# Attention's last units in an attention and feed-forward kernel: the division by the maxima in three steps, and the last norms' shift as a step of its own

## The chip, the cores and the metric

The kernel runs on one core of a Trainium2 chip. The metric is the device time of one launch in microseconds (us). The core has five engines that work side by side, each through its own instructions in order: TensorE (PE, matmuls), VectorE (DVE), ScalarE (ACT), GpSimd (POOL) and SyncE (SP), of which the last issues most of the transfers.

## The reference

Four sequences of 1024 tokens with 256 features go through attention with 16 heads of 16 features, and then through a gated feed-forward block of width 1024. Each half is normalised before and after, and added to its input.

```python
x = x + _layernorm(_L0_attn_ref(_layernorm(x, axis=-1), L0_attn_Wqkv, L0_attn_Wout), axis=-1)
x = x + _layernorm(_L0_ffn_ref(_layernorm(x, axis=-1), ...), axis=-1)

# attention's softmax
x_max = jax.lax.stop_gradient(jnp.max(x, axis=-1, keepdims=True))
exp_x = jnp.exp(jnp.clip(x - x_max, -50.0, 50.0))
return exp_x / (jnp.sum(exp_x, axis=-1, keepdims=True) + EPS)

# feed-forward
h = jax.nn.silu(_tlin(x, w1_w, w1_s)) * _tlin(x, w2_w, w2_s)
h = jax.nn.gelu(_tlin(h, h1_w, h1_s), approximate=False)
h = jax.nn.gelu(_tlin(h, h2_w, h2_s), approximate=False)
return _tlin(h, w3_w, w3_s)
```

The kernel takes the exponential of the scores without subtracting the maximum. The maximum enters only through the small EPS (1e-6) of the denominator, which must then be scaled by the largest exponential of a row: den = EPS * (largest exponential) + (sum of exponentials).

## The kernel before, in words

**Attention's units.** The work of attention is cut into 4 sequences x 4 groups of 4 heads x 2 halves of 512 queries: 32 units. A unit has 16 tiles: 8 blocks c of 128 keys, with two tiles u of two heads each. For a tile, two matmuls make the scores in a PSUM buffer `s` (L536; there are three such buffers, and the feed-forward's `pg` and `ph` use the same three), and ACT takes the exponential into a ring of SBUF buffers `e` (L537). The ring holds 8 tiles, that is 4 blocks c. `weigh` (L544) multiplies the exponentials by the values into one PSUM buffer `acc`, four matmuls for a block; a block may be cut into two halves of 256 queries. `rise` (L556) keeps the running maximum of the exponentials of a unit in `top` on VectorE, for 128 of the 512 queries: the first of a unit reads blocks 0 and 1, each later one a further block, seven in all. A part of the ring is written again only when both `weigh` and `rise` have read it.

**The end of a unit.** `unit_end` (L795) transposes `acc` into `o` (L798) and hands the division to a list of work on the side. `divide` sends the maxima through DRAM to turn them. The two units of the last sequence's last group take `divide_last` (L599) instead, which turns and folds the maxima on VectorE alone, in one step: a transpose (`turned`, L605), a reduction (L606), four small copies (L609), a reduction (L611), four small copies (`em`, L615), and the four instructions of `quotients` (L563 to L567), which end in the normalised heads `on`.

**The ending of half a sequence.** `ending` (L620) is what follows the last group of a half: two transposes to `oT` (L629), two products with the output weights, `py` (L321), each copied to `y`, then the norm of y (statistics, and `root` with POOL's power), its application and the residual's addition. In the last sequence the application is ACT's, which needs `nb`, the shift, made by VectorE in `shift` (L117) at the head of the first `apply`. All `py` use one PSUM buffer, `misc`. Behind the projections of half 1 stands `open_ffn`, which opens the feed-forward's memory.

**The list on the side.** There is no scheduler behind this: the order of every engine's instructions is the order in which the Python code emits them. The main loop emits scores, exponentials, maxima and weighings by the turn (three tiles at a time), and after each turn calls `take`, which walks through chains of steps. A `Step(run, gap, tensor, heavy, work)` may run when `gap` turns have passed since the last step of its chain; one with `work` also needs that much room on VectorE left in this turn; only one step with matmuls runs in a turn.

```python
while (step := self.due(chain, self.slot, free)) and (step.tensor or not step.work or self.room > spare):
```

**The first part of the feed-forward.** After the last unit, `gated` (L954) emits 16 groups, 8 for each half of the first sequence: eight `pg` matmuls (L966), ACT's `sg` (L968) and VectorE's `g` (L969), which frees the PSUM buffer. For the first sequence `take` is called after each group, so that attention's last steps are emitted between the groups; after the eighth everything that `open_ffn` waits for is emitted at once:

```python
steps[7].append(lambda: until(lambda: "fb" in ffn))
```

From there on, steps of the feed-forward split `g` into two parts for the next layer, `hi` on ACT (L936) and `lo` on VectorE (L940), and the `ph` matmuls (L1045) follow after group 16.

Of the kernel before, what the change touches and what calls it, by code (L numbers as in the profile page):

```python
# [19 lines left out]
P = 128  # L20
HEADS = 16
DH = 16
SLOT = 32
HPG = P // SLOT
# [15 lines left out]
TPQ = NQ // P  # L40
# [41 lines left out]
class Norms:  # L82
# [30 lines left out]
    def shift(self, stats, n=TPQ):  # L113

        mv, rstd = stats
        nb = self.small.tile([P, TPQ], F32, tag="nb", name="nb", bufs=self.bufs)
        self.nc.vector.scalar_tensor_tensor(nb[:, :n], mv[:, :n, 0], -1.0, rstd[:, :n], ALU.mult, ALU.mult)  # L117
        return rstd, nb
# [11 lines left out]
def tile_fast(ctx: ExitStack, tc: tile.TileContext, x, wqk, wv, wo, w1, w1s, w2, w2s, h1, h1s, h2, h2s, w3, w3s, out, bad):  # L130
    nc = tc.nc
    B, S, D = x.shape
# [4 lines left out]
    NH = S // NQ  # L137
# [34 lines left out]
    norms = Norms(nc, const, small)  # L172
# [23 lines left out]
    with ExitStack() as actx, ExitStack() as rctx:  # L196
# [59 lines left out]
        work = actx.enter_context(tc.tile_pool(name="work", bufs=2, side="right"))  # L256

        def misc(name):
            return ps_misc.tile([P, NQ], F32, tag="misc", name=name)
# [58 lines left out]
        def by_slots(o, w, i, **flags):  # L318

            for j in range(0, P, SLOT):  # L320
                nc.tensor.matmul(o[j : j + SLOT, :], w[:, j : j + SLOT], i, **flags)  # L321
# [236 lines left out]
        def quotients(g, h, em, o):  # L558

            o = o.rearrange("p (j s) -> p j s", s=SLOT)  # L560
            den = small.tile([P, NQ // SLOT], F32, tag="den", name="den")
            n = P // SLOT
            nc.vector.scalar_tensor_tensor(den[:, 0:n], em, SM_EPS, o[:, 0:n, DH], ALU.mult, ALU.add)  # L563
            nc.vector.tensor_copy(den[:, n:], o[:, n:, DH])
            nc.vector.reciprocal(den, den)
            e = DH * (g % GPT)
            nc.vector.tensor_mul(on[h][:, g // GPT, :, e : e + DH], o[:, :, 0:DH], den.unsqueeze(2).to_broadcast([P, NQ // SLOT, DH]))  # L567
# [31 lines left out]
        def divide_last(g, h, o, top):  # L599


            def run():
                turned = work.tile([P, P // SLOT, P], F32, tag="folded", name="turned", bufs=1)
                flat, n = top.rearrange("p u n q -> p (u n q)"), HPG * P // SLOT
                nc.vector.transpose(turned.rearrange("p s q -> p (s q)"), flat)  # L605
                nc.vector.tensor_reduce(flat[:, 0:n], turned.rearrange("p s (j k) -> p (s j) k", k=SLOT), AX.X, ALU.max)  # L606
                parts = flat[0:SLOT, n : n + n * P // SLOT].rearrange("p (k n) -> p k n", n=n)
                for k in range(P // SLOT):
                    nc.vector.tensor_copy(parts[:, k], flat[SLOT * k : SLOT * (k + 1), 0:n])  # L609
                most = flat[0:SLOT, P : P + n]  # L610
                nc.vector.tensor_reduce(most, parts.rearrange("p k n -> p n k"), AX.X, ALU.max)  # L611
                most = most.rearrange("p (i j) -> p i j", i=HPG)
                em = small.tile([P, P // SLOT], F32, tag="em", name="em")
                for i in range(HPG):
                    nc.vector.tensor_copy(em[SLOT * i : SLOT * (i + 1), :], most[:, i])  # L615
                quotients(g, h, em, o)

            return [Step(run, 1, False)]

        def ending(b, h, copy):  # L620

            st = {}

            def transposes(c):
                def run():
                    if c == 0:
                        st["oT"] = work.tile([P, DC, NQ], F32, tag="oT", name=f"oT_{b}_{h}", bufs=1)
                        st["y"] = (both if h else work).tile([P, TPQ, D], F32, tag="y", name=f"y_{b}_{h}", bufs=1)
                    nc.vector.transpose(st["oT"][:, c, :], on[h][:, c].rearrange("p j s -> p (j s)"))  # L629

                return run

            def project(t0):
                def run(*parts):
                    if 0 in parts:
                        st["py"] = misc(f"py_{b}_{h}_{t0}").rearrange("p (t d) -> p t d", d=D)
                    py = st["py"]
                    for i in parts:
                        for c in range(DC):
                            by_slots(py[:, i, :], st["oT"][:, c, (t0 + i) * P : (t0 + i + 1) * P], wo_sb[:, c, :], start=c == 0, stop=c == DC - 1)  # L640
                    if 1 not in parts:
                        return
                    (copy if b == B - 1 else to_scalar)(st["y"][:, t0 : t0 + 2, :], py)

                return run

            def gather(i):
                def run():
                    st["mv"] = norms.gather([st["y"][:, j, :] for j in range(i, i + 2)], i, st.get("mv"))

                return run

            def root():
                st["ln"] = norms.root(st["mv"])

            def apply(i0):
                def run():
                    if b == B - 1 and i0 == 0:
                        st["to"] = norms.shift(st["ln"])
                    for i in range(i0, i0 + 2):  # L660
                        if b == B - 1:
                            norms.scale(st["y"][:, i, :], st["y"][:, i, :], st["to"], i)
                        else:
                            norms.apply(st["y"][:, i, :], st["y"][:, i, :], st["ln"], i)

                return run

            def residual(i):
                def run():
                    xr = xs[b][:, h * TPQ + i : h * TPQ + i + 2, :]  # L670
                    nc.vector.tensor_add(xr, xr, st["y"][:, i : i + 2, :])

                return run

            steps = [Step(transposes(c), 1, False, work=0.7) for c in range(DC)] + [Step(lambda run=project(t): run(0, 1), 2, heavy=True) for t in range(0, TPQ, 2)]
            before = (b, h - 1) if h else (b - 1, NH - 1)
            steps[0].ready = lambda: before not in ends or not any(step.tensor for step in ends[before][0])
            tail = (
                [Step(gather(i), 1, False, work=1.6) for i in range(0, TPQ, 2)] + [Step(root, 0, False, work=0.3)]
                + [Step(apply(i), 2 if b == B - 1 and not i else 1, False, work=1.2) for i in range(0, TPQ, 2)] + [Step(residual(i), 1, False, work=1) for i in range(0, TPQ, 2)]  # L680
            )
            if b < B - 1:

                return steps + [Step(lambda: side.add(tail), 0, False)]
            opened = Step(open_ffn, 0, False)
            opened.ready = lambda: not ends[b, 0][0]
            return steps + ([opened] if h == NH - 1 else []) + tail
# [107 lines left out]
        def unit_end(b, g, h):  # L795
# [7 lines left out]
            if g == NG - 1:  # L803
                last = ending(b, h, to_scalar if (b, h) == (B - 1, NH - 1) else to_vector)
                unit[0].extend(last)
                ends[b, h] = unit
# [429 lines left out]
        def feed_forward():  # L1236
# [27 lines left out]
            for b in range(B):  # L1264
# [25 lines left out]
                until(lambda: made_factors[0] == len(corners) and "fb" in ffn)  # L1290
                q = 2 * 7 * b
                ops, extra, early = ending(one, False)
                if b == 0:
                    for g in range(3, 12):
# [8 lines left out]
                until(lambda: not chain[0])  # L1303
                two = Layer(y, ops[0, 0], ops[1, 0])
                ops, extra, early = ending(two, True)
                if b:
                    checked(extra, (3, 4), (5, 6))
# [79 lines left out]
        while weighed < len(tiles):  # L1387
            n = end = made
# [3 lines left out]
            if made == len(tiles):  # L1392
                n = made
# [8 lines left out]
            while halves and weighed + 2 <= n:  # L1402
                b, g, h, c, _ = tiles[weighed]
# [264 lines left out]
```

## Time and profile before

| | |
|---|---|
| three runs, us | 1205.09, 1205.70, 1208.14 (median 1205.7) |
| the profiled execution, us | 1206.14, of which the span from first to last instruction is 1204.4 |
| busy share of the span | TensorE 96%, ACT 74%, VectorE 70%, POOL 25% |
| granted TensorE clock, mean | 0.994 |
| last exponentials of attention | end at 576.7 us |
| first pg matmul | 577.7 us |
| first ph matmul | 617.8 us |

The profile is one execution. A line such as L556 names the kernel's line whose instruction it is. In the groups, `out<-in` are the program's names of the tiles. Idle time of an engine is put down to the instruction that ended it. The matmuls are pipelined, so their single durations overlap.

### The profile page before, as it was taken

How to read it: one execution, taken by the hardware profiler on the slowest of the kernel's cores; microseconds unless marked ns; L12 is line 12 of the kernel's file. 1: busy time of each engine (PE TensorE's matmuls, PEld its weight loads, DVE VectorE, ACT ScalarE, POOL GpSimd, SP SyncE). 2: the span in 40 equal slices, each digit the busy share in tenths (PEclk: the TensorE clock that was granted, in tenths of full speed). 3: DMA queues.
4: the chain of work that ended last, by engine and by line, in shares of the span. 5: the costliest groups of instructions: out<-in, count | busy, mean ns of one | idle time of the engine just before them, and what ended most of it. 6: DMA issues, size and time to landing. Idle time of an engine off the chain costs nothing.

```text
span 1204.4 us, 21320 instructions
## 1 busy us (share of the span) xinstructions
PE 1160.6 (96%) x7994; PEld 709.1 (59%) x7994; DVE 845.9 (70%) x1501; ACT 886.2 (74%) x1050; POOL 298.7 (25%) x458
## 2 busy tenths in 40 slices
PE   8999999999999999998999999999999999999994
PEld 3333333333333333332678889888898888988884
DVE  4577777785878867767585756867678676785765
ACT  4999888988999989998466575576756767567660
POOL 6454256565566643220000000000000000000000
PEclk9999999999999999999999999999999999999997
DMA  5877655676666664472314441354522545225401
GB/s 144 214 185 185 150 134 157 163 178 163 155 175 164 167 166 105 106 176 88 105 36 140 134 147 57 101 175 153 179 74 85 177 154 176 74 84 187 157 24 38
DMA packets 78672, 163.66 MB, mean 136 GB/s; under 512 B 14688, under 2 KB 40928, under 8 KB 78560
## 3 DMA queue, kind: packets, MB, share of 16 engines
q1 hardware_dynamic: 62832, 120.18, 34.9%
q0 software_dynamic: 15200, 41.50, 12.6%
q8 instruction: 65, 1.06, 0.4%
q10 hardware_dynamic: 528, 0.52, 0.1%
q14 instruction: 47, 0.39, 0.1%
HBM read 98.71 MB, written 29.88 MB: 107 GB/s over the span
## 4 chain that ended last, share of the span: by engine, by line
PE 71%; DVE 10%; ACT 9%; issue 4%; DMA 3%; SPq 2%; POOL 1%; ACTq 0%; POOLq 0%; DVEq 0%
PE ph L1045 35%; PE acc L544 10%; PE pg L966 9%; ACT e L537 8%; PE s L536 7%; PE pz L1153 4%; PE p L321 2%; DVE top L556 2%; PE py L321 2%; SPq L482 1%; PE pv L321 1%; DVE st L97 1%; DMA x<-in_x_dram 1%; DMA sq<-cq0hi 1%; PE fpt L909 1%
## 5 line engine op out<-in xcount | busy, mean ns | idle before, releaser
L537 ACT ACTIVATE e<-s 128x1024 f32<-128x1024 f32 x512 | 483.0, 1046 | 43.8 <-PE s L536 34.1
L544 PE MATMUL acc<-e,vaug 128*32 128x512 f32 (+1 forms) x2424 | 256.6, 535 | 1.4 <-DVE o L798 1.4
L107 POOL TENSOR_TENSOR rstd<-ve,minus_half 128x4 f32<-128x4 f32 (+1 forms) x34 | 38.3, 1126 | 700.6 <-DVE ve L105 596.2
L536 PE MATMUL s<-sq,sk 64*128 64x512 f32 x1024 | 188.9, 445 | 20.7 <-ACT e L537 19.5
L536 PEld LDWEIGHTS s<-sq,sk 64*128 64x128 f32 x1024 | 87.3, 184 | 167.9 <-ACT e L537 147.4
L1045 PE MATMUL ph<-hi,sq 128*128 128x512 f32 x448 | 177.8, 397 | 0.0
L1045 PE MATMUL ph<-lo,sq 128*128 128x512 f32 x448 | 176.7, 394 | 0.0
L1045 PE MATMUL ph<-hi,sk 128*128 128x512 f32 x448 | 176.6, 394 | 0.0
L1045 PE MATMUL ph<-lo,sk 128*128 128x512 f32 x448 | 176.5, 394 | 0.0
L556 DVE TENSOR_TENSOR top<-top,e 128x512 f32<-128x512 f32 x192 | 140.1, 730 | 21.1 <-ACT e L537 15.4
L544 PEld LDWEIGHTS acc<-e,vaug 128*32 128x32 f32 x2424 | 61.9, 109 | 117.4 <-issue 107.4
L940 DVE TENSOR_TENSOR lo<-g,hi 128x1024 fp32r<-128x1024 f32 x48 | 58.8, 1224 | 57.8 <-ACT hi L936 57.8
L1045 PEld LDWEIGHTS ph<-lo,sk 128*128 128x128 f32 x448 | 84.1, 188 | 20.0
L1045 PEld LDWEIGHTS ph<-hi,sk 128*128 128x128 f32 x448 | 84.1, 188 | 20.0
L1045 PEld LDWEIGHTS ph<-hi,sq 128*128 128x128 f32 x448 | 84.1, 188 | 19.5
L1045 PEld LDWEIGHTS ph<-lo,sq 128*128 128x128 f32 x448 | 84.2, 188 | 19.2
L1033 ACT ACTIVATE c<-ph,h_scale 128x512 f32<-128x512 f32 x64 | 40.5, 684 | 55.8 <-PE ph L1045 55.8
L940 DVE TENSOR_TENSOR lo<-c,hi 128x1024 fp32r<-128x1024 f32 x48 | 58.2, 1219 | 25.8 <-ACT hi L936 25.8
L968 ACT ACTIVATE sg<-pg,w_scale 128x512 f32<-128x512 f32 x64 | 43.9, 687 | 41.6 <-PE pg L966 38.2
L321 PE MATMUL p<-xT,wqk_sb 128*32 128x512 f32 x512 | 65.7, 593 | 0.5 <-ACT xT L324 0.5
L969 DVE SCALAR_TENSOR_TENSOR g<-pg,w_scale,sg 128x512 f32<-128x512 f32 x64 | 47.7, 747 | 22.1 <-ACT sg L968 22.1
L1153 PE MATMUL pz<-w_sb,hi 128*128 128x256 f32 x256 | 60.1, 279 | 0.0
(189 smaller groups left out, 1830.0 us busy)
## 6 DMA issues: line engine op xcount, KB each, us to landing
sq<-h_f SPq DMA_DIRECT2D x56, 512.0 KB, 3.9
sk<-h_f SPq DMA_DIRECT2D x56, 512.0 KB, 4.7
w<-in_h_dram POOLq DMA_DIRECT2D x32, 256.0 KB, 4.9
h_f<-wr POOLq DMA_DIRECT2D x16, 512.0 KB, 3.7
x<-in_h_dram SPq DMA_DIRECT2D x16, 512.0 KB, 3.6
top_d<-top SPq DMA_DIRECT2D x30, 256.0 KB, 2.5
folded<-top_d SPq DMA_DIRECT2D x30, 256.0 KB, 3.6
h_f<-wr POOLq DMA_DIRECT2D x16, 384.0 KB, 3.8
```

What stands on the lines that cost most here:

```text
L321: nc.tensor.matmul(o[j : j + SLOT, :], w[:, j : j + SLOT], i, **flags)
L536: nc.tensor.matmul(s[:, a, :], stacks[1, g % 2, u][r, c * P : (c + 1) * P], stacks[0, g % 2, u][r, h * NQ : (h + 1) * NQ], start=True, sto ...
L537: nc.scalar.activation(pair(k)[:, u], s, AF.Exp)
L544: nc.tensor.matmul(acc[SLOT * i : SLOT * (i + 1), q0:q1], vaug[g % 2][:, c, i, :], pair(k)[:, i // 2, i % 2, q0:q1], start=c == 0 and q0 = ...
L556: nc.vector.tensor_max(top, top if c > 1 else pair(k - 2)[:, :, :, 0:P], pair(k)[:, :, :, 0:P])
L940: nc.vector.tensor_sub(self.lo[i].t, self.raw[i].t, self.hi[i].t.bitcast(F32))
L966: nc.tensor.matmul(p[:, k, :], homes[n][d][:, m * P : (m + 1) * P], half[:, d, :], start=d == j == 0, stop=d == DC - 1 and j == 1)
L968: nc.scalar.activation(sg, p[:, 0, :], AF.Silu, scale=scales["w1"][:, m : m + 1])
L969: nc.vector.scalar_tensor_tensor(x[i, h][c // 2].t[:, c % 2, :], p[:, 1, :], scales["w2"][:, m : m + 1], sg, ALU.mult, ALU.mult)
L1033: nc.scalar.activation(o.t[:, j, :], (o.t if src is None else src)[:, j, :], AF.Gelu, scale=scale[:, m : m + 1])
L1045: nc.tensor.matmul(p[:, j, :], w, half, start=start and c == n == 0, stop=c == HC // 2 - 1 and n == 1, skip_group_check=True,)
L1153: nc.tensor.matmul(p[:, j, :D], half[:, (t0 + j) * P : (t0 + j + 1) * P], homes["w3"][c], start=c == order[0] and n == 0, stop=c == order[ ...
```

## The change

Two things are changed. First, `divide_last` returns three steps in place of one: `turn` (transpose and first reduction), `fold` (four copies and second reduction) and `run` (the copies to `em` and the quotients). For half 1 the second and third follow at once; for half 0 each has a gap of one turn and a weight in work. Second, in the last sequence `norms.shift` is a step of its own, `shift`, with a gap of 1 + h turns, and the first `apply` has a gap of 1 in place of 2.

```diff
         def divide_last(g, h, o, top):
-            def run():
+            flat, n = top.rearrange("p u n q -> p (u n q)"), HPG * P // SLOT
+            most = flat[0:SLOT, P : P + n]
+
+            def turn():
                 turned = work.tile([P, P // SLOT, P], F32, tag="folded", name="turned", bufs=1)
-                flat, n = top.rearrange("p u n q -> p (u n q)"), HPG * P // SLOT
                 nc.vector.transpose(turned.rearrange("p s q -> p (s q)"), flat)
                 nc.vector.tensor_reduce(flat[:, 0:n], turned.rearrange("p s (j k) -> p (s j) k", k=SLOT), AX.X, ALU.max)
+
+            def fold():
                 parts = flat[0:SLOT, n : n + n * P // SLOT].rearrange("p (k n) -> p k n", n=n)
                 for k in range(P // SLOT):
                     nc.vector.tensor_copy(parts[:, k], flat[SLOT * k : SLOT * (k + 1), 0:n])
-                most = flat[0:SLOT, P : P + n]
                 nc.vector.tensor_reduce(most, parts.rearrange("p k n -> p n k"), AX.X, ALU.max)
-                most = most.rearrange("p (i j) -> p i j", i=HPG)
+
+            def run():
                 em = small.tile([P, P // SLOT], F32, tag="em", name="em")
                 for i in range(HPG):
-                    nc.vector.tensor_copy(em[SLOT * i : SLOT * (i + 1), :], most[:, i])
+                    nc.vector.tensor_copy(em[SLOT * i : SLOT * (i + 1), :], most.rearrange("p (i j) -> p i j", i=HPG)[:, i])
                 quotients(g, h, em, o)
-            return [Step(run, 1, False)]
+            if h == NH - 1:
+                return [Step(turn, 1, False), Step(fold, 0, False), Step(run, 0, False)]
+            return [Step(turn, 1, False, work=1.4), Step(fold, 1, False, work=1.0), Step(run, 1, False, work=1.7)]
...
+            def shift():
+                st["to"] = norms.shift(st["ln"])
+
             def apply(i0):
                 def run():
-                    if b == B - 1 and i0 == 0:
-                        st["to"] = norms.shift(st["ln"])
                     for i in range(i0, i0 + 2):
...
-                + [Step(apply(i), 2 if b == B - 1 and not i else 1, False, work=1.2) for i in range(0, TPQ, 2)] + [Step(residual(i), 1, False, work=1) for i in range(0, TPQ, 2)]
+                + ([Step(shift, 1 + h, False)] if b == B - 1 else []) + [Step(apply(i), 1, False, work=1.2) for i in range(0, TPQ, 2)] + [Step(residual(i), 1, False, work=1) for i in range(0, TPQ, 2)]
```

In the order of instructions, only the stretch between the last unit's first maximum and the end of the pg groups differs. On VectorE the first maximum of the last unit follows L606, the second and third follow L611, the fourth follows L567; the second `oT` transpose of half 0 follows the first `g`. On TensorE the four `py` products follow pg groups 3, 5, 8 and 8, where they followed groups 1, 3, 6 and 8. On ACT the fourth `hi` (after group 12) stands ahead of half 1's shifts instead of behind them.

## The prediction

> **What bounds the kernel now.** I read the page's busy slices first, then the chain of work that ended last around the place that the change touches, then the timelines of ACT and TensorE there.
>
> ```profile
> PE   8999999999999999998999999999999999999994
> ACT  4999888988999989998466575576756767567660
> ```
>
> TensorE is at nine tenths nearly everywhere, so an edit can gain only where TensorE waits. The one 8 behind the start is the slice from 542 to 572 us, the end of attention; ACT falls from 8 to 4 behind it. There the chain reads (start, us, what):
>
> ```profile
> 563.06 0.63 DVE turned L605
> 563.72 0.70 DVE top L606
> ...
> 565.17 0.26 DVE top L611
> ...
> 567.08 0.69 DVE top L556
> ...
> 568.77 0.72 ACT e L537
> ```
>
> The path to the end runs through the whole of one division (L605 to L567), then through one running maximum (L556), then to ACT's exponentials. The waits of 556 to 612 us name it (us in total, times, longest), and the timelines of ACT and TensorE show both ends (in brackets the idle time before an instruction, and who ended it):
>
> ```profile
> ACT e L537 <- DVE top L556: 3.9, 1, 3.9
> ```
>
> ```profile
> 567.85 5.61 ACT L537 ACTIVATE e<-s 128x1024 f32<-128x1024 f32 x6 [3.92 <-DVE top L556]
> 574.73 1.94 ACT L537 ACTIVATE e<-s 128x1024 f32<-128x1024 f32 x2 [1.27 <-PE s L536]
> ...
> 568.93 0.50 PE L536 MATMUL s<-sq,sk 64*128 64x512 f32 x2 [2.85 <-ACT e L537]
> ```
>
> ACT has filled the ring of eight tiles of e by 563.94. The ninth tile overwrites the first, which the first maximum of the last unit reads; that maximum stands on VectorE behind the 15 instructions of the other half's division. So ACT is idle for 3.92 us, then TensorE, starved of s buffers, for 2.85. Stretches of 1 us (length, then busy us of TensorE, its weight loads, VectorE, ACT and POOL, then the granted clock) show a second price:
>
> ```profile
> 570.00:571.00 1.00, 0.59 (x4) 0.23 (x4) 0.94 (x2) 1.00 (x2) 0.00 (x0) 0.94 0.00 0
> 571.00:572.00 1.00, 1.00 (x10) 0.37 (x12) 0.34 (x1) 1.00 (x2) 0.00 (x0) 0.50 0.06 16
> ...
> 574.00:575.00 1.00, 1.00 (x12) 0.52 (x12) 0.18 (x1) 0.27 (x1) 0.00 (x0) 0.85 0.00 0
> ```
>
> The clock is at half speed from about 570.9 to 574.3. Sixteen weighing matmuls (L544) take 2.79 us there and 1.50 at 564.58, and ACT waits another 1.27 us for s. The last weighing ends and the first pg matmul of the feed-forward starts at 577.77. From there to the first ph matmul at 617.95 is 40.18 us, with TensorE idle in two places:
>
> ```profile
> 611.11 0.51 PE L966 MATMUL pg<-ck1hi,ck0hi 128*128 128x512 f32 x1 [0.96 <-DVE g L969]
> 615.82 0.50 PE L966 MATMUL pg<-ck1hi,ck0hi 128*128 128x512 f32 x1 [0.75 <-DVE g L969]
> ...
> 611.82 1.09 ACT L122 ACTIVATE y<-y,nb,rstd 128x256 f32<-128x256 f32 x2 [2.99 <-DVE nb L117]
> ```
>
> After 617.95 the chain is TensorE alone up to the last few us, so whatever is won or lost before it shifts the end by as much.
>
> **The change part by part.** No instruction is added or removed on any engine, and no DMA is issued by the moved steps; the instruction orders of SP and POOL are as before. Up to the reduction at 563.72 (L606) all engines have the same order, so 0 there. Two stretches differ.
>
> *Part 1, the division of half 0 in three steps.* On VectorE the first maximum of the last unit now follows L606 directly; the next two follow L611; the fourth follows the division. L606 ends at 563.72 + 0.69 = 564.41, so the maximum ends at 564.44 + 0.69 = 565.1 instead of 567.8. Its inputs are there (exponentials done at 563.94), and the other reader of the ring's first pair, the weighing of c = 0, ran at 561.8 to 562.8. ACT restarted 0.09 us after the maximum, so now at 565.2: 2.65 us earlier. The second maximum ends at 565.1 + 0.7 (L609) + 0.3 (L611) + 0.7 = 566.8, the third at 567.5; they free the tiles that ACT wants at 568.9 and 570.7, so neither holds it.
>
> Then eight exponentials. Six took 5.61, that is 0.915 a step, so eight take 7.44 and end at 572.65 if s keeps up. TensorE's order is unchanged: three s tiles, each behind an exponential, the last ending at 568.6; 1.5 us of weighing at full clock to 570.1; the s of the last two tiles by 570.4 and 570.8, against ACT's wish at 570.7 and 571.6. No gap. Before, the last exponential ended at 574.73 + 1.94 = 576.67, so ACT ends 4.0 us earlier. The last weighing follows 1.1 us behind, as before: first pg at 573.7 instead of 577.8. Of the 4.0, 2.65 is the wait and 1.35 is what the half clock cost.
>
> That second term rests on the clock staying up. In the trace the half clock begins 4.8 us after TensorE's pause began, behind a 3.4 us stretch (567.5 to 570.9) in which it was busy for about 1.3 us, 37%. The Trainium skill ("TensorE: Matmul & The Clock Gate", "What's actually happening" and "HAM oscillation — how this bites in real kernels") says that the clock drops to half after at least one idle window of about 3.4 us, and comes back after one busy window. Read strictly, a pause of 2.85 us is too short, the half clock has another cause and stays: then part 1 is worth 2.65. The row speaks for the pause: it dropped in the window that held it, and for 3.4 us. In the new order TensorE is busy about 2.5 of the 3.4 us from 566.1 (1.5 for three s tiles, 0.95 of weighing), 74%, and an earlier row had less without a drop:
>
> ```profile
> 22.00:26.00 4.00, 2.29 (x26) 1.18 (x18) 0.29 (x1) 1.96 (x3) 3.99 (x9) 1.00 0.56 125
> ```
>
> 57% at clock 1.00. I take 4.0 and keep 2.65 as the other end.
>
> *Part 2, the order inside the pg stage.* The second oT transpose now stands behind the first g (L969), so the four py products come behind pg groups 3, 5, 8 and 8 instead of 1, 3, 6 and 8; the two of half 1 are pushed out together at group 8 by the wait for the feed-forward's pool. I count from the first pg, p. Durations from the rows: three groups 5.66, one py 1.86, a division 4.1 (582.36 to 586.45), g and copies 0.65 a step.
> VectorE: g1 ends at p+3.5, oT 4.1, division 8.2, g2 8.9, g3 9.5, y 10.1. TensorE: first py at 5.7 (oT there), groups 4 and 5 from 7.5 and 9.55 (they need g1 and g2: margins 4.0 and 0.65), second py at 11.4 (needs the y copy, 10.1), groups 6 to 8 to 18.9. The third py needs the last transpose at 18.5: margin 0.4. So nothing waits until here.
> New wait: the fourth py uses the one misc buffer that the third just filled; ACT's copy (L324, 0.60) must end first. TensorE idles 0.65 us and ends the py at 23.3, against 22.9 before (fewer changes between pg and py give some back).
> Then ACT does copy, two pairs of shifts (L122), and hi, which ends at 25.9; the nb it needs (ve, POOL's pow at 1.0, nb) is there at about 21.8. VectorE's run from the first lo to g11 took 603.25 to 611.0 = 7.75, so g11 at 33.7: group 14, ready at 32.65, waits 1.1 (before 0.96). The wait of 0.75 before group 16 goes: it came from ACT's last hi standing behind shifts that waited 2.99 us for nb (L117); now this hi is ahead of them and g13 is done at 36.4, before group 16 at 37.7. Groups end at 39.5 to 39.7, against 40.18: a gain of 0.6.
>
> *The shift as its own step.* nb is the same single 0.15 us instruction; its new place is contained in the order above.
>
> Sum: 4.0 + 0.6 = 4.6 us. The profiled execution took 1206.14 (span 1204.4, 1.7 around it): 1201.5, span 1199.8. The median of the runs is 0.44 lower than it, 1205.7: 1201.1.
>
> **The rivals.**
> *The clock drops anyway* (or the half clock was never the pause's). For: the page's rule read strictly. Against: 74% busy, and the 57% row. Gain 2.65 + 0.6 = 3.3: 1202.4.
> *The pg stage takes some back.* Three margins there are 0.65 us or less; if VectorE is late on each, groups 5 and 14 and the third py wait in turn, 0.5 to 1 us each. Part 2 then loses 1 to 2 instead of gaining 0.6: 1202.7 to 1203.7.
> *No gain at the ring.* If ACT's true releaser at 567.85 were another, near in time, part 1 is about 0. Against: the 15 VectorE instructions fill the gap without a hole. 1205 to 1206.
> *Slower.* One mechanism: the release of pg buffers by VectorE. All of VectorE from the first lo to nb stands between groups 11 and 16, and each us by which ACT's first hi comes later than p+25.9 (behind two py copies and four shifts that wait for nb) is a us of waiting before group 14. To be over 0.3% slower this must cost more than 4.0 + 3.6 = 7.6 us, so hi beyond p+33; nothing that I find delays nb so far, since POOL took 1.0 and 1.9 us for pow. At 10 us late: 1211.
>
> **How the numbers follow.** A measurement can tell about 0.3% (3.6 us) from no change: faster is below 1202.1, slower above 1209.3. Main case 0.63 (1199.6 to 1202.1, the low end if the wait before group 14 goes as well); clock drops 0.14, of which a fifth still falls below 1202.1; pg stage gives back 0.11; no gain 0.06; slower 0.06. Faster 0.66, same 0.28, slower 0.06. The range 1199.6 to 1204.0 leaves out the last two and little more.
>
> **What would show it.** Right: ACT's wait for DVE top near 564 us falls from 3.92 to about 1.3; no half clock there; first pg at 573.7; an idle of about 0.65 us before the second of two adjacent py; no wait before group 16; first ph near 613.3. Wrong: granted clock of 0.50 near 570 (term of 1.35); groups 5 or the third py waiting for DVE (margins); a first ph that comes earlier while the span does not (the claim that TensorE alone carries the rest).

## The result, and the profile after

In runs side by side the kernel before took 1207.68 us (median of 8, 1205.09 to 1210.02) and the changed kernel 1203.16 us (median of 8, 1201.04 to 1204.87). The ratio is 0.9962, with a 95% interval of 0.9952 to 0.9972: 4.5 us less, against 4.6 predicted. The absolute forecast of 1201.1 was built on three runs with a median of 1205.7; the larger set has the same kernel 2 us higher, and that is the distance between 1201.1 and 1203.2. The forecast's limit for a gain that can be told from no change, 3.6 us, lies at 1204.1 when it is counted from 1207.68, and the changed kernel is under it.

The span of the profiled execution went only from 1204.4 to 1202.5. The rest is in a part that the change doesn't touch: VectorE's last copy from `fpt` to `ck1hi` (L327) starts at 561.69 us before and at 564.29 after, behind the same instructions in the same order. In the profiles of all kernels below this first stretch took 561.4 to 566.1 us, so spans of single profiles aren't to be compared. I cut each profile into three stages that start behind it: the **pause stage**, from that copy to the first pg matmul; the **pg stage**, from there to the first ph matmul; and the **last stage**, from there to the end of the span.

| us | pause stage | pg stage | last stage | sum |
|---|---|---|---|---|
| before | 16.02 | 40.08 | 586.61 | 642.71 |
| after | 11.89 | 39.60 | 586.72 | 638.21 |
| difference | -4.13 | -0.48 | +0.11 | -4.50 |

The sum of the stages agrees with the difference of the medians. The first two stages of both kernels read as follows, before and then after (the stretch, its length, the busy us and number of instructions of TensorE, its weight loads, VectorE, ACT and POOL, then the granted clock and the share and rate of the DMA engines):

```profile
561.69:577.71 16.02, 12.26 (x91) 3.66 (x89) 10.88 (x27) 10.81 (x12) 0.00 (x0) 0.89 0.12 29
577.71:617.79 40.08, 38.37 (x259) 27.32 (x258) 28.51 (x62) 19.03 (x30) 2.92 (x2) 1.00 0.19 68
```

```profile
564.29:576.18 11.89, 10.88 (x91) 3.40 (x89) 10.01 (x26) 10.71 (x12) 0.00 (x0) 1.00 0.18 50
576.18:615.78 39.60, 37.93 (x258) 27.49 (x257) 29.79 (x64) 19.46 (x30) 2.92 (x2) 1.00 0.19 66
```

The first expectations below call the pause stage A and the pg stage B and take their ends from the chain of work instead of the timeline: their 16.08, 11.96, 40.18 and 39.70 are the 16.02, 11.89, 40.08 and 39.60 of the table.

In ACT's timeline after, the stall of 3.92 us has become 1.16, and the eight exponentials run without a second gap:

```profile
567.70 7.44 ACT L537 ACTIVATE e<-s 128x1024 f32<-128x1024 f32 x8 [1.16 <-DVE top L556]
```

VectorE's timeline after shows why. The first maximum (L556) stands right behind the first reduction of the division (L608, which was L606), ahead of the copies (L613):

```profile
566.32 0.69 DVE L608 TENSOR_REDUCE top<-turned 128x16 f32<-128x512 f32 x1
566.93 0.68 DVE L556 TENSOR_TENSOR top<-e,e 128x512 f32<-128x512 f32 x1
567.53 0.69 DVE L613 COPY top<-top 32x16 f32<-32x16 f32 x4
```

Stretches of 1 us show the granted clock at 1.00 throughout. In the kernel before it stood at 0.50 from about 9.2 to 12.6 us behind the copy to `ck1hi`, which would be 573.5 to 576.9 here:

```profile
570.00:571.00 1.00, 0.59 (x4) 0.19 (x2) 0.92 (x7) 1.00 (x2) 0.00 (x0) 1.00 0.03 8
571.00:572.00 1.00, 1.00 (x18) 0.42 (x16) 0.93 (x5) 1.00 (x2) 0.00 (x0) 1.00 0.06 16
...
573.00:574.00 1.00, 1.00 (x10) 0.29 (x12) 0.90 (x3) 1.00 (x2) 0.00 (x0) 1.00 0.08 16
574.00:575.00 1.00, 1.00 (x14) 0.36 (x8) 0.46 (x1) 1.00 (x2) 0.00 (x0) 1.00 0.89 250
```

The chain of work that ended last no longer goes through the copies and the second reduction of the division; it takes the maximum, ACT, the last scores and the weighing:

```profile
566.93 0.69 DVE top L556
...
570.61 0.49 PE s L536 x2
571.11 1.43 PE acc L544 x16
...
573.20 3.05 PE acc L544 x24
576.25 5.71 PE pg L973 x24
```

In the pg stage, TensorE's timeline has two waits as before, but one of them is another: the new one stands before the fourth `py`, the one before group 14 is unchanged, and the one before group 16 is gone:

```profile
597.77 1.93 PE L321 MATMUL py<-wo_sb,oT 128*32 128x256 f32 x32 [0.72 <-ACT y L324]
...
610.19 0.50 PE L973 MATMUL pg<-ck1hi,ck0hi 128*128 128x512 f32 x1 [0.96 <-DVE g L976]
```

### The profile page after: what moved, and what is told of

It reads as the page before. It is cut to its first block, busy times and chain, and to the rows that moved or that the text cites. A ratio compares the mean times of both kernels' runs of the same rounds, so it can differ in the third digit from the quotient of the medians.

```text
span 1202.5 us, 21319 instructions
## 1 busy us (share of the span) xinstructions
PE 1159.5 (96%) x7994; PEld 709.1 (59%) x7994; DVE 841.6 (70%) x1501; ACT 886.9 (74%) x1050; POOL 297.2 (25%) x458
## 3 DMA queue, kind: packets, MB, share of 16 engines
q0 software_dynamic: 15200, 41.50, 12.6%
## 4 chain that ended last, share of the span: by engine, by line
PE 71%; DVE 9%; ACT 8%; DMA 4%; issue 3%; POOL 2%; SPq 1%; ACTq 0%; POOLq 0%; DVEq 0%
PE ph L1052 35%; PE acc L544 10%; PE pg L973 9%; ACT e L537 7%; PE s L536 7%; PE pz L1160 4%; PE p L321 2%; DVE top L556 2%; PE py L321 2%; PE pv L321 2%; SPq L482 1%; DVE st L97 1%; DMA w<-in_h_dram 1%; DMA folded<-top_d 1%; PE fpt L916 1%
## 5 line engine op out<-in xcount | busy, mean ns | idle before, releaser
L107 POOL TENSOR_TENSOR rstd<-ve,minus_half 128x4 f32<-128x4 f32 (+1 forms) x34 | 38.5, 1131 | 697.0 <-DVE ve L105 592.6
L556 DVE TENSOR_TENSOR top<-top,e 128x512 f32<-128x512 f32 x192 | 137.7, 717 | 18.5 <-ACT e L537 12.4
L975 ACT ACTIVATE sg<-pg,w_scale 128x512 f32<-128x512 f32 x64 | 44.0, 688 | 44.1 <-PE pg L973 37.7
```

Of the source, the lines that this page charges most:

```text
L556: nc.vector.tensor_max(top, top if c > 1 else pair(k - 2)[:, :, :, 0:P], pair(k)[:, :, :, 0:P])
L975: nc.scalar.activation(sg, p[:, 0, :], AF.Silu, scale=scales["w1"][:, m : m + 1])
```

## The experiments

**The two parts apart.** The first kernel has the three steps, with the shift back at the head of the first `apply`; the second has the shift as a step, with the division in one.

```diff
 # three steps alone, against the changed kernel
-                + ([Step(shift, 1 + h, False)] if b == B - 1 else []) + [Step(apply(i), 1, False, work=1.2) ...
+                + [Step(apply(i), 2 if b == B - 1 and not i else 1, False, work=1.2) ...
```

> Only the division in three steps; the shift stays at the head of the first apply. Stage A runs from VectorE's last copy of fpt to ck1hi before the division (L327) to the first pg matmul: 16.08 us before, 11.96 in the changed kernel. Stage B runs from the first pg to the first ph matmul: 40.18 before, 39.70 in the changed kernel. Theory (the three steps bring the first maximum forward and free ACT's ring): A 11.96, and B 40.4, because the wait of 0.75 us before pg group 16 comes back, with the shifts of half 1 ahead of the fourth hi. In all 3.9 us less than before. Rival (the shift's own step carries the gain): A 16.08, total as before.

Measured: 1203.44 us (5 runs) against 1208.07, ratio 0.9961 (0.9948 to 0.9975). Pause stage 11.88, pg stage 40.63, last stage 586.63. The whole gain of the pause stage is here, but the pg stage is 0.55 longer than before, 0.3 more than expected. The device times don't tell this kernel from the changed one (ratios of 0.9961 and 0.9962); the stages do. TensorE's timeline of this kernel has three waits:

```profile
597.30 1.93 PE L321 MATMUL py<-wo_sb,oT 128*32 128x256 f32 x32 [0.72 <-ACT y L324]
609.71 0.50 PE L975 MATMUL pg<-ck1hi,ck0hi 128*128 128x512 f32 x1 [0.96 <-DVE g L978]
614.43 0.50 PE L975 MATMUL pg<-ck1hi,ck0hi 128*128 128x512 f32 x1 [0.79 <-DVE g L978]
```

```diff
 # the shift step alone, against the kernel before
             def apply(i0):
                 def run():
-                    if b == B - 1 and i0 == 0:
-                        st["to"] = norms.shift(st["ln"])
 # and the list of steps as in the changed kernel; divide_last as before
```

> Only the shift as a step of its own; the division stays one step. Theory: A 16.08, ACT's wait of 3.9 us for the maximum and the half clock stay; B 39.4, because the fourth hi stands ahead of the shifts of half 1 and the wait of 0.75 us before group 16 goes. In all 0.7 us less, which the clock time alone can't tell from nothing. Rival (the shift carries the gain): A 12, or B shorter by 4.

Measured: 1206.9 us (21 runs), ratio 0.9991 (0.9984 to 0.9998). Pause stage 15.86 with ACT's wait of 3.92 in it, pg stage 38.98, last stage 586.56. Of TensorE's waits in the pg stage only one is left:

```profile
611.27 0.50 PE L967 MATMUL pg<-ck1hi,ck0hi 128*128 128x512 f32 x1 [0.93 <-DVE g L970]
```

So the shift step is worth 1.0 to 1.1 us in the pg stage (40.08 to 38.98; with the three steps 40.63 to 39.60), more than the 0.75 listed as the wait that it removes. The timeline before shows most of the rest: pg matmuls start 0.23 us apart, but the last one before a wait runs its full 0.39, and the second one after it starts 0.34 behind the first. A listed wait of 0.75 thus costs 0.75 + 0.16 + 0.11 = 1.0. The split into three steps costs 0.55 in that stage. The changed kernel's 0.48 is the difference of the two.

**Is the half clock TensorE's pause?** The kernel before, with ten extra matmuls into the spare buffer `misc`, at the place in TensorE's order where the pause is. They compute nothing that is used.

```diff
                 weigh(weighed, accs[b, g, h], q0, q1)
+                if (b, g, h, c, q0) == (B - 1, NG - 1, NH - 1, 3, 0) and q1 < NQ:
+                    fill(10)   # nc.tensor.matmul(dummy, <64x128 of sk>, <64x512 of sq>)
```

> The kernel before with ten matmuls added in TensorE's pause (128x512, operands of the scores, result read by nothing), about 2.3 us of work, so that TensorE is not idle while ACT waits for the maximum. Theory (the half clock comes from the pause): ACT still waits 3.9 us, but the clock stays at 1.00, the wait of ACT of 1.27 us goes, A 14.7, total 1.35 us less although work was added. Rival (the half clock is not the pause's): clock 0.50 from about 571 as before, A 16.1 or more.

Measured: pause stage 14.65, 1.37 less than before, with ACT's wait where it was; pg stage 40.11, last stage 586.81; 1207.23 us (13 runs), ratio 0.9991 (0.9982 to 0.9999). ACT's timeline, and three of the stretches of 1 us (on this profile's time the half clock would have stood between about 571.4 and 574.8):

```profile
568.41 7.44 ACT L537 ACTIVATE e<-s 128x1024 f32<-128x1024 f32 x8 [3.92 <-DVE top L556]
```

```profile
572.00:573.00 1.00, 1.00 (x16) 0.24 (x8) 0.69 (x1) 1.00 (x3) 0.00 (x0) 1.00 0.08 16
573.00:574.00 1.00, 1.00 (x12) 0.46 (x12) 0.00 (x0) 1.00 (x3) 0.00 (x0) 1.00 0.00 0
574.00:575.00 1.00, 1.00 (x12) 0.26 (x8) 0.69 (x1) 1.00 (x3) 0.00 (x0) 1.00 0.18 66
```

Filling the pause with useless work keeps the clock at 1.00 and wins 1.37 us while ACT still stands for 3.92. The half clock belongs to the pause, and the pause stage's 4.13 is two terms: 2.76 of ACT's wait (3.92 to 1.16) and 1.37 of clock.

**Is it the splitting, or only where the first maximum stands?** The kernel before, with half 0's division uncut in one step, but two turns after its predecessor instead of one.

```diff
-            return [Step(run, 1, False)]
+            return [Step(run, 1 if h == NH - 1 else 2, False)]
```

> The kernel before with one number changed: the division of half 0 stays in one step, but its gap is two turns, so that the whole of it follows the first maximum of the last unit, and the second and third maximum follow it. Theory (what counts is where the maxima stand against the ring, not that the division is cut): ACT's wait at the ninth tile goes, one of about 0.95 us comes before the thirteenth, which needs the second maximum; A about 11.6, clock 1.00, B 40.2, in all 4.4 us less, a little better than the changed kernel's stage A. Rival (the uncut division just moves the stall to the second maximum): A 15 to 16, no gain.

Measured: 1202.09 us (5 runs), ratio 0.995 (0.9936 to 0.9963). Pause stage 11.58, pg stage 40.07, last stage 586.56. One number in one line gains 0.3 us more in the pause stage than the three steps, and doesn't have their cost in the pg stage, since TensorE's order is that of the kernel before. Its three stages add up to 638.21 us, the same as those of the whole change. ACT's wait is shorter than expected:

```profile
565.82 3.78 ACT L537 ACTIVATE e<-s 128x1024 f32<-128x1024 f32 x4 [0.28 <-PE s L536]
570.06 3.77 ACT L537 ACTIVATE e<-s 128x1024 f32<-128x1024 f32 x4 [0.47 <-DVE top L556]
```

What pays is that the first maximum of the last unit stands ahead of the division's copies (here ahead of the whole division). The cut into steps isn't needed for it.

**The new wait of the changed kernel, and the wait before group 14.** Two kernels, each the changed one with one edit and each executed once. In the first the fourth `py` uses the PSUM buffer of `acc`, which is free by then, instead of `misc`; in the second the statistics of half 1's y come six turns later instead of one.

```diff
 # the fourth py in acc's buffer
-                        st["py"] = misc(f"py_{b}_{h}_{t0}").rearrange(...)
+                        last = (b, h) == (B - 1, NH - 1) and t0
+                        st["py"] = (ps_acc.tile([P, NQ], F32, tag="acc", name="py_acc") if last else misc(...)).rearrange(...)
```

> The changed kernel with the fourth py in the PSUM bank of acc, which is free by then, so that it need not wait until ACT has copied the third out of misc. In the changed kernel that wait is 0.72 us and stage B (first pg to first ph) 39.60. Theory (the wait is on the path, because ACT's copy, the shifts and the first hi follow the fourth py): the wait goes, VectorE's run of lo and g starts 0.7 us earlier too, the wait before group 14 stays 0.96, B 38.9. Rival (VectorE's run hangs on nb, not on the py): the 0.7 us turn up before group 14 (1.7), B 39.6.

Measured: pause stage 11.88, pg stage 38.83, last stage 586.71 (one run, 1205.01 us). The wait of 0.72 before the fourth `py` is gone, and the pg stage is 0.77 shorter than the changed kernel's: the split's cost in that stage was the single buffer.

```diff
 # half 1's statistics later
-                [Step(gather(i), 1, False, work=1.6) ...
+                [Step(gather(i), 6 if (b, h, i) == (B - 1, NH - 1, 0) else 1, False, work=1.6) ...
```

> The changed kernel with the statistics of half 1's y six turns later, so that on VectorE they stand behind g14 instead of between g9 and g11. Theory (the wait of 0.96 us before group 14 is VectorE's backlog of two statistics of 1.2 us each ahead of g11): the wait goes, with it a restart of TensorE of some 0.15, B 38.5 in place of 39.60, and the rest (586.7 after the first ph) unchanged. Rival (something else ends late in its place, a g further on, or the ph matmuls wait for the statistics' followers): B 39.6, or the rest longer by 1.

Measured: pause stage 11.88, pg stage 38.06 (38.5 was expected) with no wait before group 14, as expected. But the last stage was 589.19, about 2.5 us longer than in the kernels so far (one run, 1205.46 us). The expectation's rival had allowed 1 us for it, by waits, but the profile lists no wait of TensorE in that stage.

**The parts that pay, together.** The first kernel joins the later division in one step with the shift step; the second adds the late statistics.

> The kernel before with the division of half 0 in one step two turns late, and the shift as its own step: the two edits that measured A 11.58 and B 38.98 alone. Theory (they touch different waits, so they add): A 11.6, B 39.0, in all 5.5 us less than before, 1 us less than the changed kernel. Rival (they do not add, since each moves VectorE's order in the pg stage): B 39.6 to 40.1, 4.4 us less than before.

Measured: 1201.38 us (6 runs) against 1209.41, ratio 0.9942 (0.9929 to 0.9956). Pause stage 11.58, pg stage 39.02, last stage 586.86: the two edits add up.

> The same, with the statistics of half 1's y six turns later as well. Theory: A 11.6, B 37.9 (the wait before group 14 goes too, 0.93 and a restart of 0.15), rest unchanged, in all 6.6 us less than before, ratio about 0.9945. Rival: another wait in the pg stage takes the place, B 39, ratio about 0.9955.

Measured: 1203.09 us (6 runs), ratio 0.9953 (0.9938 to 0.9967). Pause stage 11.58, pg stage 37.49, last stage 589.18: 1.5 won and 2.3 lost.

**Where the last stage lost 2.4 us.** The profiles with and without late statistics list no wait of TensorE there, the granted clock is 0.99 in both, and TensorE's order is the same; its single matmuls are longer. What differs is where tiles lie in SBUF: the pool of the feed-forward gives an address to each name when it is first used, and with late statistics the small tiles of the norms are named behind seven of the `hi` and `lo` halves instead of among them. Two kernels tell place from order. The first is the one with late statistics, with the names asked for in the old order when the pool opens; the second is the changed kernel, with the names asked for in the order of the late statistics.

```diff
             norms.small, norms.bufs = fb, 6
+            for tag in "mv st b0 ve rstd b1 b2 b3 nb b4".split():            # old places
+            # or "b0 b1 b2 b3 b4 b5 b6 mv st b7 ve rstd b8 ... b13 nb"       # moved places
+                shape, bufs = shapes.get(tag, ([P, 2, NQ], 1))
+                fb.tile(shape, F32, tag=tag, name=tag, bufs=bufs)
```

> This is the kernel of e11 (the kernel before, with half 0's division in one step two slots later, the shift of the last norms as a step of its own, and half 1's statistics six slots late), with one edit: the small tiles of the norms are named in the pool fb at the points where the kernel before first names them, so that every hi and lo half, every g and every z lies at the same address of SBUF as in the kernel before. No instruction is added, and the order on TensorE, VectorE and ScalarE is that of e11. Theory that e11's longer last stage (589.2 us from the first ph to the end against 586.7) comes from where the tiles lie: pause stage 11.6, pg stage 37.5, last stage back at 586.7 (586.4 to 587.0), TensorE's sum of busy time there down by about 2.5 us, in all some 2.4 us less than e11 and 1.5 us less than e10: a ratio near 0.9935 (0.9920 to 0.9950). Rival, that the late statistics themselves (their order, what they leave for later) are the cause: the last stage stays at 589.2 and the ratio at 0.9953 as with e11.

Measured: 1200.35 us (6 runs) against 1207.94, ratio 0.9936 (0.9916 to 0.9956). Pause stage 11.58, pg stage 37.49, last stage 586.74. Of the kernels timed in more than one execution it has the lowest ratio and the shortest stages, 635.81 us in sum against 638.21 of the changed kernel; the intervals of their ratios overlap a little.

> This is the changed kernel, with one edit: the small tiles of the norms and the halves of the feed-forward pool are named in the order in which e11 first names them, so that the hi and lo halves lie where they lie in e6 and e11 (169376 becomes 168992, 223200 becomes 223008 and so on: 192 to 768 bytes lower). No instruction is added, and the order on TensorE, VectorE and ScalarE is that of the changed kernel. Theory that the place of the tiles sets the pace of the last stage: pause stage 11.9, pg stage 39.6, last stage 589.2 us in place of 586.7, all of it longer matmuls of ph and pz (medians up by 1 to 3 ns): about 2.5 us more than the changed kernel, a ratio near 0.9985 (0.997 to 1.000). Rival, that the late statistics are the cause: the last stage at 586.7 and the ratio at 0.9962 as with the changed kernel.

Measured: 1205.81 us (20 runs), ratio 0.9977 (0.9969 to 0.9986). Pause stage 11.88, pg stage 39.57, last stage 588.96. With the instruction order of the changed kernel, other addresses alone take 2.2 us of the 4.5 that its stages had gained. The two views of the last stage (the stretch, its length, TensorE's busy us first), of the late statistics at the old places, and of the changed kernel at the moved ones:

```profile
610.46:1197.20 586.74, 570.22 (x2739) 472.60 (x2737) 404.69 (x534) 358.97 (x458) 16.77 (x17) 0.99 0.37 121
```

```profile
616.04:1205.00 588.96, 572.73 (x2739) 474.24 (x2737) 403.34 (x528) 357.40 (x454) 14.87 (x16) 0.99 0.37 120
```

Equal counts of matmuls, 2.5 us more of busy time. The groups by tile (busy us in total, mean ns of one) put it on the matmuls that read the halves; a group of pg, which doesn't read them, keeps its time, and so the clock isn't the cause. First the changed kernel as it is, then with the places moved (the pg groups are those of the last stage alone):

```profile
L1052 PE MATMUL ph<-lo,sk 128*128 128x512 f32 x448 | 176.4, 394 | 0.0
L1160 PE MATMUL pz<-w_sb,hi 128*128 128x256 f32 x256 | 60.1, 279 | 0.0
L973 PE MATMUL pg<-ck1hi,ck0hi 128*128 128x512 f32 x24 | 9.3, 389 | 0.0
```

```profile
L1056 PE MATMUL ph<-lo,sk 128*128 128x512 f32 x448 | 177.4, 396 | 0.0
L1164 PE MATMUL pz<-w_sb,hi 128*128 128x256 f32 x256 | 61.0, 282 | 0.0
L977 PE MATMUL pg<-ck1hi,ck0hi 128*128 128x512 f32 x24 | 9.3, 389 | 0.0
```

Two more kernels ask what about the place counts. Both are the one with late statistics at the old places with one edit, and each was executed once: in the first all addresses of the pool are 32 bytes lower, in the second all the halves lie side by side.

```diff
 # 32 bytes lower: after all other names of the pool
+            fb.tile([P, 8], F32, tag="pad", name="pad", bufs=1)
 # side by side
-            for tag in "mv st b0 ve rstd b1 b2 b3 nb b4".split():
+            for tag in "b0 b1 b2 b3 b4 b5 b6 b7 b8 b9 b10 b11 b12 b13 mv st ve rstd nb".split():
```

> The kernel of e12 with one unused tile of 32 bytes named last in the pool fb, so that its halves, its small tiles and w3_sb all lie 32 bytes lower (169376 becomes 169344): the distances between them stay, and their addresses become multiples of 64. The order on TensorE, VectorE and ScalarE is that of e12. If the distances between the tiles of this pool set the pace of the last stage, it stays at 586.7 us; if it is the alignment to 64 bytes, it moves: shorter (below 586) if aligned tiles read faster, 589 if slower. Pause stage 11.6 and pg stage 37.5 in all cases.

Measured: pause stage 11.59, pg stage 37.49, last stage 584.88 (one run, 1201.92 us, beside 1208.93 of the kernel before). The last stage is 1.9 us shorter than at the old places. Not all of its matmuls gained: in the mean, the four groups of ph fell by 1 to 2 ns, but those of pz rose from 279 to 280 ns. The whole stage reads:

```profile
615.22:1200.10 584.88, 568.14 (x2739) 473.09 (x2737) 404.85 (x534) 358.93 (x458) 16.78 (x17) 0.99 0.36 121
```

> The kernel of e12 with the small tiles of the norms behind all 14 halves of the pool fb, so that these lie side by side, 4096 bytes apart, from 168992 to 222240. The order on TensorE, VectorE and ScalarE is that of e12. If gaps between the halves (384 to 960 bytes in the kernel before) are what keeps the matmuls short, the last stage is at 589.2 us or above, since seven of the halves lay side by side in e13 and all do here; if only single addresses matter, it can be anything from 586.7 to 589.2. Pause stage 11.6 and pg stage 37.5.

Measured: pause stage 11.59, pg stage 37.49, last stage 589.07 (one run, 1202.53 us).

Neither theory of the expectations stands alone, then. If only the distances inside the pool counted, the shift by 32 bytes would have changed nothing; if only the alignment to 64 bytes counted, the moved places would have changed nothing, since the halves lie there by multiples of 64 bytes lower than at the old ones (192 to 960 bytes; the expectation had 768 as the most). The shift doesn't show that alignment is what counts: it also changed the distances to the tiles outside the pool, such as `sq` and `sk`, which ph reads together with the halves. In the nine profiles with the old places the last stage took 586.56 to 586.86 us, in the three with the moved ones 588.96 to 589.19, so a difference of 1.9 is far outside what one profile leaves uncertain. Why a place is fast stays open. The stages of the kernel with all addresses lower add up to 633.96 us, 8.75 less than the kernel before, but this is one execution.

## Why the prediction was right, point by point

- **ACT's wait for the first maximum.** Expected to fall from 3.92 to about 1.3, worth 2.65; it is 1.16, worth 2.76. The three steps alone have it (1.17 in that kernel), the shift step alone has not.
- **Eight exponentials without a gap in 7.44 us.** They took 7.44. The last scores don't hold ACT.
- **The half clock, 1.35.** It went, and the filled pause gives its price as 1.37 with nothing changed but the added matmuls. Here the prediction had to choose between the row and the Trainium skill ("TensorE: Matmul & The Clock Gate", "What's actually happening"), which asks for an idle window of about 3.4 us. Measured, a pause of 2.85 us was enough, with TensorE busy for 37% of the 3.4 us before the drop, and filling the pause prevented it. The measurement decides, though no run tells at which share the clock drops; the other end of the estimate, 2.65 for this part, would have been 1.5 too low.
- **The first pg matmul.** Expected 12.0 us after the start of the last copy to `ck1hi` (573.7 against 561.69); measured 11.89.
- **The pg stage, 0.6.** Measured 0.48. Its margins held: no wait before group 5 and none before the third `py`. The new wait before the fourth `py` was 0.72 (0.65 expected), the one before group 14 was 0.96 as before (1.1 expected), and the one before group 16 went. The count from the first pg came out close: group 14 was expected at 33.7 us and group 16 at 37.7, and they started at 34.0 and 37.8. The listed waits so went only from 1.71 to 1.68 us. The gain is in TensorE's busy time of the stage, 38.37 to 37.93 us. The two parts alone show where it comes from: with the three steps, where two `py` follow each other with no pg group between, it is 38.16, and with the shift step, where a wait for g and the matmul that drains ahead of it are gone, 38.05. The prediction named the first only in passing ("give some back") and didn't price it.
- **The shift step itself, 0.** This term was put in the wrong place, with no effect on the sum. The prediction saw that the fourth `hi` now stands ahead of the shifts, and that the wait before group 16 goes, but booked this to the order as a whole. By itself the step is worth 1.1 us, and the three steps by themselves cost 0.55 in that stage.
- **The last stage, 0.** 586.61 and 586.72. What was won before it stayed won. The first ph was expected near 613.3; it started 51.49 us behind the copy to `ck1hi`, which is 613.2 on the time of the profile before. That it depends on where the tiles lie was in no part of the prediction; the change moved none of them.
- **The rivals.** The clock didn't drop; ACT's wait fell as the first maximum came earlier, so no other releaser held the ring; the pg stage gave nothing back in sum, though the three steps alone do (0.55, less than the 1 to 2 of that rival); the release of pg buffers by VectorE cost 0.96 before group 14, as it had before.

## What to carry to other kernels

When an engine stalls on a small instruction that stands in line behind a long run of work which nobody awaits, try to move the whole run behind it before cutting it: one changed gap gave 4.4 us here where three steps gave 4.1 and cost 0.55 later. Price a pause of TensorE by its length and by the clock that follows it, and a short wait by what the drained pipeline adds to it. And when an edit moves the first use of a tile's name, compare the tiles' addresses too: a stage with no change in its instructions can change its length.

## What the runs showed of the hardware that I had not expected

- **The place of operands in SBUF sets the pace of matmuls by some tenths of a per cent.** With one and the same order of instructions, the last stage took 584.88, 586.74 and 589.07 us by the addresses alone; in the changed kernel the 512-column matmuls of ph that read `sk` went from 394 to 396 ns on average, and those of pz, 256 columns wide, from 279 to 282, when the places moved. Over the stage's 2739 matmuls this is 2.5 us of busy time, more than half of what the whole change gained. The cause is not known.
- **A pause of 2.85 us was enough to halve the clock.** Its matmuls restarted at full speed, but 4.8 us after the pause began, with TensorE idle for about 63% of the last 3.4 us, 3.4 us at half speed followed; the kernel with the shift step alone, which has a pause of 2.9 us there, dropped to 0.50 too. 2.56 us of matmuls laid into the pause kept the clock at 1.00.
